# A layer of state space and experts: edge decays in four matmuls, routing and sends cut into pieces of the chunk steps, first expert weights asked two pieces sooner

## The chip, the core and the metric

The kernel runs on one core of a Trainium2 chip. Its engines are TensorE (PE, matmuls and transposes), VectorE (DVE), ScalarE (ACT), GpSimd (POOL) and SyncE (SP, which here only issues transfers). The metric is the device time of one execution in microseconds (us), smaller is better. A kernel's time is the median of its runs; the profile shows one further execution.

## The reference

Two layers over 8 sequences of 512 tokens of width 256, all in float32. Layer 0 normalizes `x`, then adds two things to it: a bidirectional state space block (projection, a convolution of 4 taps, a scan over chunks of 128 tokens with 8 heads and both directions, a gate, an output projection) and a mixture of 8 experts in which every token goes to its best one. Layer 1 normalizes again and adds latent attention of 16 heads and a second mixture with two experts per token. Of layer 0, cut to what the change touches:

```python
# state space: A = -exp(A_log), dt = softplus(proj + dt_bias); per chunk and direction
A_cs = cumsum(A * dt)                     # over the 128 tokens of the chunk
Y = C B^T * exp(segsum(A*dt)) (x*dt)  +  C state * exp(A_cs)    # inside the chunk, and from the state
# experts
probs = softmax(xn @ Wr + br); gate = max(probs); idx = argmax(probs)
y = gate * (relu(xn @ W1[idx] + b1[idx]) @ W2[idx] + b2[idx])
```

`exp(A_cs)` is what the kernel calls the edge decay (`ex`): with it the carried state enters every token of a chunk.

## The kernel before

**Opening.** `norm_and_project` goes over the 8 sequences, normalizes the tokens into `xn`, keeps the transposed ones in DRAM (`xtd`), and projects them onto `dt` and the router's logits (`proj`). `route` then computes `dt` and `da` (the product with A), and routes the tokens: softmax, first maximum, `ranks` (two matmuls and a sum over the 32 token tiles), the slot of every token (`slot0`) and the expert of every block of 128 slots (`w_idx`). It ends with 32 indirect transfers from GpSimd (L407), the "sends": each writes 128 rows of `xn` to their slots in the DRAM tensor `xd0`. Next come the first sequence's convolution parts, `decays` (L418 to L425), the first two chunks' preparation, and `edges` (L427 to L438): for each sequence and direction four matmuls into 8 rows, an exponential, and a write to the DRAM tensor `exd`, from which a chunk reads its edge decays (`ex`, L841). `edges` takes its rows `e8` from the rotating buffers `row` (8 of them), which also hold the rows of the convolution and the token rows `xt`.

The opening is put in order by a scheduler.

**Chunk steps.** Under `manual_schedule` every engine gets its instructions in the order in which the program states them. There are 64 steps n, 8 per sequence; j is n % 8. Each step does one chunk of one direction: `segments` and `prepare` for the next ones (`seg`, `au`), `inside` (`yd`), `before` (`yoff`, `ex`, added to `yT`), `pairs` (`cbm`, `xdd`), `behind` (the state `st`), `weigh` (`mt`). `others(n)` adds, in up to three turns, work of the neighbouring sequences: convolution parts of the next one (`pj`, `cv`, `th`; j = 1 to 6), gate, norm and output of the last one (j = 0 to 4), tokens (`xp`, `xt`, `xdt`, `bp`; j = 7 and 0).

Between these calls, `fill(1)` takes one piece of the experts: the generator `blocks` has 39 blocks of 128 slots, and a block is five pieces: transposes of its rows (L474, copy L476), first product in two halves (`h_ps`, L486, evicted by ScalarE at L493 and by VectorE at L495), second product in two halves (`y_ps`, L499), the last with the bias and the write to `yd0`. `fetch(j)` reads a block's rows from `xd0` through SP (L457) and its weights `w1`, `w2` and biases `b12` by indirect transfers from GpSimd (L461); it is called for block j + 1 in the first piece of block j. There are four calls of `fill` in a step, from step 2 on. When the blocks are done, `fill` takes pieces of `late`, the opening of layer 1: weights, then per finished sequence four gathers (`yg`), and seven pieces which add the experts' result, normalize again (`xn`, L567), transpose (`tp`, L575) and project. The last eight steps have two more calls.

```python
                if begun:
                    fill(1)          # begun = n >= 2; four times in a step
```

**Layer 1** interleaves attention steps with its own routing, sends, experts and gathers; the change doesn't touch it.

Of the kernel before, what the change touches and what calls it, by code (L numbers as in the profile page):

```python
# [8 lines left out]
FP = mybir.dt.float32  # L9
I32 = mybir.dt.int32  # L10
AF = mybir.ActivationFunctionType
ALU = mybir.AluOpType
# [37 lines left out]
def bc(ap, axis, shape):  # L50

    return ap.unsqueeze(axis).to_broadcast(shape)
# [3 lines left out]
def tile_kernel(ctx: ExitStack, tc: tile.TileContext, t, out: bass.AP):  # L56
# [48 lines left out]
    xtd = dram.tile([B, P, KC, S], FP, name="xtd", tag="xtd")  # L105
    exd = dram.tile([B, 2, NH, S], FP, name="exd", tag="exd")
    fdd = dram.tile([B, NH, S], FP, name="fdd", tag="fdd")
# [202 lines left out]
    dt = l0c.tile(D3, FP, name="dt", tag="dt")  # L310
    da = l0c.tile(D3, FP, name="da", tag="da")
    gate = ctile("gate", [P, NTILE])
# [3 lines left out]
    dec_tok = l0c.tile([P, 2, NTILE, NH], FP, name="dec_tok", tag="dec_tok")  # L316
    dec_all = l0c.tile(D3, FP, name="dec_all", tag="dec_all")

# [5 lines left out]

    def route():
        pool, big = r0p, r0b
        proj = big.tile([P, NTILE, 2 * NH + NE], FP, name="proj0", tag="proj0")
        xTs = {}
# [65 lines left out]
        V.tensor_copy(slot0, slots_of(big, oh, rank, "a"))  # L394


        B3 = [P, NBLK, NE - 1]
# [4 lines left out]
        V.tensor_scalar(be, be, float(P), pidx, ALU.mult, ALU.add)  # L402
        V.tensor_copy(w_idx, be)

        sent = []
        for i in range(NTILE):
            one = G.indirect_dma_start(  # L407
                out=xd0, out_offset=bass.IndirectOffsetOnAxis(ap=slot0[:, i : i + 1], axis=0),
                in_=xn[:, i, :], in_offset=None, bounds_check=NBLK * P - 1, oob_is_err=False,
            )  # L410
            for other in sent:
                tc.declare_no_dep(one.ins, other.ins, reason="rows go to slots of their own")
            sent.append(one)

    def decays():
        dp = bank("dp", [P, 2, NTILE * NH], 0)
        for d in range(2):
            T.matmul(  # L418
                dp[:, d, :].rearrange("p (t h) -> p t h", h=NH), LOW[d], da[:, :, d * NH : (d + 1) * NH],
                start=True, stop=True,  # L420
            )
        A.activation(dec_tok.rearrange("p d t h -> p d (t h)"), dp, AF.Exp)
        ta = bank("ta", [P, NTILE * 2 * NH], 0)
        T.matmul(ta, ones, da.rearrange(f2), start=True, stop=True)
        A.activation(dec_all.rearrange(f2), ta, AF.Exp)  # L425

    def edges():  # L427
        for b in range(B):
            for d in range(2):
                ct = bank("ct", [NH, S], 0)  # L430
                for c in range(TPB):
                    T.matmul(
                        ct[:, c * P : (c + 1) * P], da[:, b * TPB + c, d * NH : (d + 1) * NH], MSK[d],
                        start=True, stop=True,
                    )
                e8 = row("e8")
                A.activation(e8[:NH, :], ct, AF.Exp)
                Y.dma_start(out=exd[b, d], in_=e8[:NH, :])  # L438

    route()  # L440
    l1c = tl = w_r = rb = w_q = w_o = w_uk = w_uv = w_kv = band = slot1 = wsel = proj1 = vt0 = qk0 = r1b = noop = None
# [4 lines left out]
    with ExitStack() as es:  # L446
# [7 lines left out]

        def fetch(j):
            xd = e2.tile([P, DM], FP, name="xd", tag="xd", bufs=3)
            Y.dma_start(out=xd, in_=xd0[j * P : (j + 1) * P, :])  # L457
            got = [xd]
            for name, n, bufs in (("w1", KC * FF, 2), ("w2", FC * DM, 2), ("b12", FC + DM, 2)):
                w = e2.tile([P, n], FP, name=name, tag=name, bufs=bufs)  # L460
                G.indirect_dma_start(  # L461
                    out=w, out_offset=None, in_=t[name], bounds_check=NE * P - 1, oob_is_err=False,
                    in_offset=bass.IndirectOffsetOnAxis(ap=w_idx[:, j : j + 1], axis=0),
                )
                got.append(w)
            return got

        def blocks():
            got = fetch(0)
            for j in range(NBLK):  # L470
                xd, w1, w2, b12 = got
                tp = bank("xdT_ps", [P, DM], "e")
# [3 lines left out]
                A.copy(xdT, tp)  # L476
                if j + 1 < NBLK:
                    got = fetch(j + 1)
                yield
# [342 lines left out]
        class Chunk:  # L822
# [9 lines left out]
            def prepare(self):  # L832
                d = self.d
                self.au = p1.tile(H3, FP, name="au", tag="au")
                G.tensor_tensor(  # L835
                    self.au, bc(da[:, self.i, d * NH : (d + 1) * NH], 2, H3), bc(MSK[d], 1, H3), ALU.mult
                )
                if not self.first:
                    self.ex = p2.tile([P, HC, P], FP, name="ex", tag="ex", bufs=3)
                    for i in range(2):  # L840
                        Y.dma_start(  # L841
                            out=self.ex[HD * i : HD * (i + 1), :, :],
                            in_=bc(exd[self.b, d, i::2, self.cols], 0, [HD, HC, P]),
                        )
# [55 lines left out]
            def behind(self):  # L900
                if self.last:
                    return
                sp = bank("sp", [P, DI], "s")
                T.matmul(sp, self.bt.b_tok[self.c][:, self.d, :], self.xdd, start=True, stop=True)
                st = state[self.d]
                if self.first:
                    A.copy(st, sp)
                else:
                    d = self.d
                    G.tensor_tensor(  # L910
                        heads(st), heads(st), bc(dec_all[:, self.i, d * NH : (d + 1) * NH], 2, HP), ALU.mult
                    )
                    V.tensor_tensor(st, st, sp, ALU.add)
# [37 lines left out]
        batch[1].load()  # L951
        r0.close()
        xs.close()
        e2 = es.enter_context(tc.tile_pool(name="e2", bufs=2, side="right"))

        with tc.manual_schedule(engines=ENGINES):
# [31 lines left out]

            rows, rest = blocks(), late()

# [5 lines left out]
            for n in range(N):  # L996
# [6 lines left out]
                ahead = chunk[n + 1] if n + 1 < N else None  # L1003
                begun = n >= 2

# [14 lines left out]
                if begun:  # L1020
                    fill(1)
                now.before()
                if ahead:
                    ahead.pairs(batch[ahead.b])
                if begun:
                    fill(1)
# [4 lines left out]
                if begun:  # L1031
                    fill(1)
                while work:
                    turn()
                if n >= N - 8:
                    fill(2)
# [512 lines left out]
```

## Time and profile before

| | |
|---|---|
| median of 3 runs | 2250.88 us (2246.86 to 2252.46) |
| the profiled execution | 2233.12 us, span 2231.4 us, mean granted TensorE clock 0.922 |
| TensorE busy | 1935.2 us, 87% of the span |
| VectorE, ScalarE, GpSimd busy | 1499.0, 1070.2 and 689.8 us |
| 56 to 112 us | TensorE 33.2 of 56 us busy, clock 0.82; VectorE 44.6; GpSimd 5.7 |
| 112 to 168 us | TensorE 30.3 of 56 us busy, clock 0.73; VectorE 20.5; GpSimd 39.2 |
| 168 to 224 us | TensorE 51.9 of 56 us busy, clock 0.97 |
| 235 to 937 us | TensorE 668.6 of 702 us busy, clock 0.99 |
| 937 to 1175 us | TensorE 182.4 of 238 us busy, clock 0.84 |

The span runs from the first to the last instruction of one execution. The first chunk step begins at 169.8 us (its `yd`), block 0's first product at 191.4, the last block ends in step 50 near 944, the last step's `yd` is at 1147, and layer 1's first scores are at 1174.7. In a timeline line the columns are start, duration, engine, line, operation, out<-in, shape and count, and in brackets how long the engine was idle before it and what ended that. A matmul's end is modelled, so start-to-start distances are the better measure of what it costs TensorE. In a line of waits the numbers are the total in us, how often, and the longest.

### The profile page before, as it was taken

What the parts mean: (1) busy time and instruction counts of PE and PEld (TensorE: products, weight loads), DVE (VectorE), ACT (ScalarE), POOL (GpSimd) and SP (SyncE); (2) the same over time, 40 slices, a digit from 0 to 9 for tenths busy, and PEclk for the clock granted to TensorE, in tenths of its full rate; (3) what the DMA queues carried; (4) which work ended last, traced back from release to release, by engine and by line L of the source; (5) the groups of instructions that cost most, each with busy time, mean ns of one, the idle gap of its engine ahead of it and who ended that gap; (6) DMA issues with size and microseconds to landing.
All of it is one profiled execution on the core that took longest, in us unless ns stands there. A gap on an engine that the chain in (4) does not pass through costs nothing. (4 is left out here: it accounts for less than half of the span.)

```text
span 2231.4 us, 32949 instructions
## 1 busy us (share of the span) xinstructions
PE 1935.2 (87%) x11772; PEld 1281.0 (57%) x11772; DVE 1499.0 (67%) x3323; ACT 1070.2 (48%) x1978; POOL 689.8 (31%) x588
## 2 busy tenths in 40 slices
PE   6559999999998999987867768899999999999885
PEld 5325666667766676644544334565656656565543
DVE  4835766657585665678646679565666767676895
ACT  2223332323233242333324546676667777777764
POOL 0075554546364463655420035200000000000452
PEclk9879999999999999997885878799999999999978
DMA  7134544545454464343432161312213222222255
GB/s 263 38 103 160 174 157 162 193 141 203 139 172 150 132 212 143 128 128 114 157 100 67 37 212 61 96 53 84 71 46 101 82 67 78 58 86 58 90 110 97
DMA packets 156357, 263.61 MB, mean 118 GB/s; under 512 B 25146, under 2 KB 112622, under 8 KB 144290
## 3 DMA queue, kind: packets, MB, share of 16 engines
q1 hardware_dynamic: 124544, 144.65, 20.9%
q0 software_dynamic: 22320, 107.55, 14.9%
q10 hardware_dynamic: 9330, 9.31, 1.2%
q8 instruction: 93, 1.52, 0.3%
q14 instruction: 70, 0.57, 0.1%
HBM read 193.39 MB, written 72.75 MB: 119 GB/s over the span
## 5 line engine op out<-in xcount | busy, mean ns | idle before, releaser
L1289 DVE TENSOR_SCALAR s<-s_ps 128x512 f32<-128x512 f32 x512 | 317.4, 681 | 255.9 <-PE s_ps L1284 209.0
L1299 ACT ACTIVATE s<-s,ng 128x512 f32<-128x512 f32 x512 | 355.3, 727 | 51.7 <-DVE ng L1295 50.1
L1306 PE MATMUL p_ps<-ident,s 128*128 128x128 f32 x2048 | 296.0, 289 | 60.5 <-ACT pT L1307 60.5
L1306 PEld LDWEIGHTS p_ps<-ident,s 128*128 128x128 f32 x2048 | 244.7, 147 | 143.7 <-ACT pT L1307 94.3
L1291 DVE CUSTOM_DVE_ANT_0 s<-s,band 128x512 f32<-128x512 f32 x512 | 322.3, 683 | 0.0
L1307 ACT COPY pT<-p_ps 128x512 f32<-128x512 f32 x512 | 277.8, 591 | 56.3 <-PE p_ps L1306 52.1
L1249 POOL DMA_INDIRECT yg<-yd,at x64 | 67.6, 1056 | 700.6 <-PE s_ps L1284 654.3
L667 PE MATMUL pj<-xT,w_in 128*128 128x512 f32 x384 | 194.6, 632 | 19.4 <-DVE cv L680 18.3
L1284 PE MATMUL s_ps<-kT,qT 16*128 16x512 f32 x1024 | 181.5, 706 | 22.6 <-DVE s L1289 16.5
L486 PEld LDWEIGHTS h_ps<-xdT,w 128*128 128x128 f32 x1248 | 151.6, 195 | 32.6 <-issue 18.0
L486 PE MATMUL h_ps<-xdT,w 128*128 128x128 f32 x1248 | 156.7, 280 | 9.4 <-ACT xdT L476 8.3
L499 PE MATMUL y_ps<-w,hT 128*128 128x256 f32 x624 | 149.3, 382 | 0.7 <-DVE hT L495 0.7
L680 DVE SCALAR_TENSOR_TENSOR cv<-pj,w_conv_w,cv 128x511 f32<-128x511 f32 (+2 forms) x192 | 143.1, 745 | 7.4 <-ACT cv L676 3.4
L1315 PE MATMUL o_ps<-pT,vt 128*32 128x256 f32 x2048 | 143.2, 424 | 0.0
L898 POOL TENSOR_TENSOR yT<-yT,ex 128x512 f32<-128x512 f32 (+1 forms) x48 | 59.4, 1237 | 254.1 <-DVE ex L897 191.6
L499 PEld LDWEIGHTS y_ps<-w,hT 128*128 128x128 f32 x624 | 116.9, 192 | 35.7 <-issue 20.3
L887 DVE TENSOR_TENSOR yT<-yT,yd 128x512 f32<-128x512 f32 (+1 forms) x64 | 43.7, 682 | 122.6 <-PE yd L878 122.5
L667 PEld LDWEIGHTS pj<-xT,w_in 128*128 128x128 f32 x384 | 71.6, 200 | 92.1 <-issue 81.9
L1151 PE MATMUL e_hp<-e_xdT,e_w 128*128 128x256 f32 x448 | 122.4, 396 | 2.3 <-ACT e_xdT L1145 1.9
L835 POOL TENSOR_TENSOR au<-da,row_le 128x1024 f32<-128x1024 f32 x32 | 62.5, 1954 | 195.0 <-DVE end L387 94.1
L1164 PE MATMUL e_yp<-e_w,e_hT 128*128 128x256 f32 x448 | 120.0, 390 | 0.2
L855 ACT ACTIVATE mt<-seg 128x1024 f32<-128x1024 f32 x64 | 65.6, 1024 | 106.7 <-PE seg L850 106.6
(261 smaller groups left out, 3219.0 us busy)
## 6 DMA issues: line engine op xcount, KB each, us to landing
ex<-exd SPq DMA_DIRECT2D x96, 128.0 KB
u<-in_u_dram SPq DMA_DIRECT2D x16, 512.0 KB
xtd<-xT SPq DMA_DIRECT2D x16, 512.0 KB
fr<-fdd SPq DMA_DIRECT2D x64, 128.0 KB
od<-os SPq DMA_DIRECT2D x32, 256.0 KB
xT<-xtd SPq DMA_DIRECT2D x15, 512.0 KB
e_w<-in_ei_dram SPq DMA_DIRECT2D x7, 1024.0 KB
e_w<-in_eo_dram SPq DMA_DIRECT2D x7, 1024.0 KB
```

The costliest lines, as they stand in the source:

```text
L486: T.matmul(hp[:, i, :], w1[:, k * FF + f * P : k * FF + (f + 1) * P], xdT[:, k * P : (k + 1) * P], start=(k == 0), stop=(k == KC - 1),)
L499: T.matmul(yp, hT[f // 4][:, f % 4, :], w2[:, f * DM : (f + 1) * DM], start=(f == 0), stop=(f == FC - 1))
L667: T.matmul(pj, w_in[:, k, o * P : (o + 1) * P], self.xT[:, k, :], start=(k == 0), stop=(k == KC - 1))
L680: V.scalar_tensor_tensor(cv[:, s:], pj[:, : S - s], conv_w[:, q, 3 - s : 4 - s], cv[:, s:], ALU.mult, ALU.add)
L1151: T.matmul(hp, w1[:, k, f * P : (f + 1) * P], xdT[:, k, :], start=(k == 0), stop=(k == KC - 1))
L1284: T.matmul(sp[i], self.q[r, cols], self.k[r, :], start=True, stop=True)
L1289: V.tensor_scalar(self.p[i], sp[i], -CLAMP, CLAMP, ALU.max, ALU.min)
L1291: V.tensor_tensor_reduce(out=self.p[i], in0=self.p[i], in1=band[:, at : at + S], scale=1.0, scalar=-3.0e38, op0=ALU.mult, op1=ALU.max, acc ...
L1299: A.activation(self.p[i], self.p[i], AF.Exp, bias=self.ng[:, i : i + 1])
L1306: T.transpose(pp[:, k, :], self.p[i][:, k * P : (k + 1) * P], ident)
L1307: A.copy(pT[i][:, :, cc * P : (cc + 1) * P], pp)
L1315: T.matmul(op[32 * i : 32 * i + 32, half * 2 * P : (half + 1) * 2 * P], self.v[:, k, h * (AD + 1) : h * (AD + 1) + 32], pT[i][:, k, :], st ...
```

## The change

1. `da` and `dec_all` change their layout from token tile by direction and head to direction by token tile by head. One multiplication becomes two.
2. `edges` makes, for each direction and half of the token tiles, one matmul with 128 columns (16 tiles by 8 heads) into one bank; one exponential and one write follow. `exd` has the new layout, and L841 reads it there.
3. `route` is split: `steps` keeps the projection, `dt` and `da`; `route0` is a generator with the routing in six pieces and the sends in 16 pieces of two. The two matmuls of `ranks` use a bank of the experts' kind.
4. `fill` takes `route0`'s pieces first, then those of `blocks`. It is called in every step from 0 on, and a fifth time, at the end, in the first three steps of each sequence (j < 3). The pools of the opening are closed and the experts' pool opened inside `blocks`.
5. `fetch` asks by name. Block j + 1's `b12` and `w2` are asked for in the first piece of block j, as before; the rows and `w1` of block j + 2 in the fourth piece of block j, which is two pieces sooner than before.

```diff
+    exd = dram.tile([4, P, P], FP, name="exd", tag="exd")
+    EDGE = P // NH
...
-    da = l0c.tile(D3, FP, name="da", tag="da")
+    da = l0c.tile([P, 2, NTILE, NH], FP, name="da", tag="da")
...
-        V.tensor_tensor(da, dt, bc(ea, 1, D3), ALU.mult)
+        for d in range(2):
+            of = slice(d * NH, (d + 1) * NH)
+            V.tensor_tensor(da[:, d], dt[:, :, of], bc(ea[:, of], 1, [P, NTILE, NH]), ALU.mult)
+
+    def route0():
+        big = r0b
         pr = softmax_experts(big, proj[:, :, 2 * NH :], br)
+        yield
         m, oh = first_max(big, pr, "a")
         V.tensor_copy(gate, m)
-        rank, n = ranks(big, bank, oh)
+        yield
+        rank, n = ranks(big, lambda name, shape, tag: bank(name, shape, "e"), oh)
+        yield
...
         for i in range(NTILE):
...
+            if i % 2:
+                yield
...
     def edges():
-        for b in range(B):
-            for d in range(2):
-                ct = bank("ct", [NH, S], 0)
-                for c in range(TPB):
-                    T.matmul(
-                        ct[:, c * P : (c + 1) * P], da[:, b * TPB + c, d * NH : (d + 1) * NH], MSK[d],
-                        start=True, stop=True,
-                    )
-                e8 = row("e8")
-                A.activation(e8[:NH, :], ct, AF.Exp)
-                Y.dma_start(out=exd[b, d], in_=e8[:NH, :])
+        ct = bank("ct", [P, 4, P], 0)
+        for d in range(2):
+            for g in range(2):
+                T.matmul(
+                    ct[:, 2 * d + g, :], da[:, d, EDGE * g : EDGE * (g + 1), :].rearrange("p t e -> p (t e)"), MSK[d],
+                    start=True, stop=True,
+                )
+        e8 = row("e8").rearrange("p (g l) -> p g l", l=P)
+        A.activation(e8, ct, AF.Exp)
+        Y.dma_start(out=exd.rearrange("g p l -> p g l"), in_=e8)
...
         def blocks():
-            got = fetch(0)
+            nonlocal e2
+            r0.close()
+            xs.close()
+            e2 = es.enter_context(tc.tile_pool(name="e2", bufs=2, side="right"))
+            fetch(0, "xd", "w1", "b12", "w2")
+            fetch(1, "xd", "w1")
+            yield
             for j in range(NBLK):
...
-                if j + 1 < NBLK:
-                    got = fetch(j + 1)
+                fetch(j + 1, "b12", "w2")
                 yield
...
                     if f == 3:
+                        fetch(j + 2, "xd", "w1")
                         yield
...
-            rows, rest = blocks(), late()
+            rows, rest = itertools.chain(route0(), blocks()), late()
...
-                begun = n >= 2
...
-                if begun:
-                    fill(1)
+                fill(1)
...
                 while work:
                     turn()
+                if n % 8 < 3:
+                    fill(1)
```

More of the change, by code (lines that the diff above doesn't have):

```diff
@@ L1 @@
+import itertools
 from contextlib import ExitStack
@@ L105, in tile_kernel @@
     xtd = dram.tile([B, P, KC, S], FP, name="xtd", tag="xtd")
-    exd = dram.tile([B, 2, NH, S], FP, name="exd", tag="exd")
+    exd = dram.tile([4, P, P], FP, name="exd", tag="exd")
+    EDGE = P // NH
     fdd = dram.tile([B, NH, S], FP, name="fdd", tag="fdd")
@@ L316, in tile_kernel @@
     dec_tok = l0c.tile([P, 2, NTILE, NH], FP, name="dec_tok", tag="dec_tok")
-    dec_all = l0c.tile(D3, FP, name="dec_all", tag="dec_all")
+    dec_all = l0c.tile([P, 2, NTILE, NH], FP, name="dec_all", tag="dec_all")
     def bank(name, shape, tag="gen"):
@@ L323, in row, with steps @@
         return m2.tile([P, S], FP, name=name, tag="row", bufs=8)
-    def route():
+    proj = r0b.tile([P, NTILE, 2 * NH + NE], FP, name="proj0", tag="proj0")
+    def steps():
         pool, big = r0p, r0b
-        proj = big.tile([P, NTILE, 2 * NH + NE], FP, name="proj0", tag="proj0")
         xTs = {}
@@ L403, in route @@
         V.tensor_copy(w_idx, be)
+        yield
         sent = []
@@ L413, in route @@
             sent.append(one)
+            if i % 2:
+                yield
     def decays():
@@ L418, in decays @@
             T.matmul(
-                dp[:, d, :].rearrange("p (t h) -> p t h", h=NH), LOW[d], da[:, :, d * NH : (d + 1) * NH],
+                dp[:, d, :].rearrange("p (t h) -> p t h", h=NH), LOW[d], da[:, d],
                 start=True, stop=True,
@@ L423, in decays @@
         ta = bank("ta", [P, NTILE * 2 * NH], 0)
-        T.matmul(ta, ones, da.rearrange(f2), start=True, stop=True)
-        A.activation(dec_all.rearrange(f2), ta, AF.Exp)
+        T.matmul(ta, ones, da.rearrange("p d t e -> p (d t e)"), start=True, stop=True)
+        A.activation(dec_all.rearrange("p d t e -> p (d t e)"), ta, AF.Exp)
     def edges():
-        for b in range(B):
-            for d in range(2):
-                ct = bank("ct", [NH, S], 0)
-                for c in range(TPB):
-                    T.matmul(
-                        ct[:, c * P : (c + 1) * P], da[:, b * TPB + c, d * NH : (d + 1) * NH], MSK[d],
-                        start=True, stop=True,
-                    )
-                e8 = row("e8")
-                A.activation(e8[:NH, :], ct, AF.Exp)
-                Y.dma_start(out=exd[b, d], in_=e8[:NH, :])
-    route()
+        ct = bank("ct", [P, 4, P], 0)
[8 more added lines that the diff above has]
+        Y.dma_start(out=exd.rearrange("g p l -> p g l"), in_=e8)
+    steps()
     l1c = tl = w_r = rb = w_q = w_o = w_uk = w_uv = w_kv = band = slot1 = wsel = proj1 = vt0 = qk0 = r1b = noop = None
@@ L452, in heads, with fetch @@
             return ap.rearrange("p (h e) -> p h e", e=HD)
[L455 to L466, printed above, removed]
-        def blocks():
-            got = fetch(0)
+        def fetch(j, *names):
+            if j < NBLK:
+                for name in names:
+                    n, bufs = {"xd": (DM, 3), "w1": (KC * FF, 2), "w2": (FC * DM, 2), "b12": (FC + DM, 2)}[name]
+                    w = held[name, j] = e2.tile([P, n], FP, name=name, tag=name, bufs=bufs)
+                    if name == "xd":
+                        Y.dma_start(out=w, in_=xd0[j * P : (j + 1) * P, :])
+                    else:
+                        G.indirect_dma_start(
+                            out=w, out_offset=None, in_=t[name], bounds_check=NE * P - 1, oob_is_err=False,
+                            in_offset=bass.IndirectOffsetOnAxis(ap=w_idx[:, j : j + 1], axis=0),
+                        )
+        held = {}
+        def blocks():
+            nonlocal e2
[4 more added lines that the diff above has]
+            fetch(1, "xd", "w1")
+            yield
             for j in range(NBLK):
-                xd, w1, w2, b12 = got
+                xd, w1, w2, b12 = (held.pop((name, j)) for name in ("xd", "w1", "w2", "b12"))
                 tp = bank("xdT_ps", [P, DM], "e")
@@ L835, in prepare @@
                 G.tensor_tensor(
-                    self.au, bc(da[:, self.i, d * NH : (d + 1) * NH], 2, H3), bc(MSK[d], 1, H3), ALU.mult
+                    self.au, bc(da[:, d, self.i, :], 2, H3), bc(MSK[d], 1, H3), ALU.mult
                 )
@@ L839, in prepare @@
                     self.ex = p2.tile([P, HC, P], FP, name="ex", tag="ex", bufs=3)
+                    at = self.i % EDGE * NH
                     for i in range(2):
@@ L842, in prepare @@
                             out=self.ex[HD * i : HD * (i + 1), :, :],
-                            in_=bc(exd[self.b, d, i::2, self.cols], 0, [HD, HC, P]),
+                            in_=bc(exd[2 * d + self.i // EDGE, at + i : at + NH : 2, :], 0, [HD, HC, P]),
                         )
@@ L910, in behind @@
                     G.tensor_tensor(
-                        heads(st), heads(st), bc(dec_all[:, self.i, d * NH : (d + 1) * NH], 2, HP), ALU.mult
+                        heads(st), heads(st), bc(dec_all[:, d, self.i, :], 2, HP), ALU.mult
                     )
@@ L951, in tile_kernel @@
         batch[1].load()
-        r0.close()
-        xs.close()
-        e2 = es.enter_context(tc.tile_pool(name="e2", bufs=2, side="right"))
+        e2 = None
         with tc.manual_schedule(engines=ENGINES):
@@ L1015, in tile_kernel @@
                     pending.append(beginning)
-                if begun:
-                    fill(1)
+                fill(1)
                 now.inside()
                 turn()
-                if begun:
-                    fill(1)
+                fill(1)
                 now.before()
@@ L1024, in tile_kernel @@
                     ahead.pairs(batch[ahead.b])
-                if begun:
-                    fill(1)
+                fill(1)
                 turn()
@@ L1030, in tile_kernel @@
                     ahead.weigh()
-                if begun:
-                    fill(1)
+                fill(1)
                 while work:
                     turn()
+                if n % 8 < 3:
+                    fill(1)
                 if n >= N - 8:
```

## The prediction

> **What bounds the kernel now.** I read the page's slices first, then the timeline of each engine from 70 to 250 us (where the moved work lies), then TensorE's waits over the chunk steps, then one chunk step in detail. In the 40 slices (55.8 us each) TensorE is nearly full from slice 4 to 16; the holes are slices 1 and 2 and the stretch after slice 16.
>
> ```profile
> PE   6559999999998999987867768899999999999885
> POOL 0075554546364463655420035200000000000452
> PEclk9879999999999999997885878799999999999978
> ```
>
> TensorE's timeline shows what fills slice 2, and where the steps begin:
>
> ```profile
> 141.17 1.04 PE L432 MATMUL ct<-row_ge,da 128*8 128x128 f32 x8
> 158.05 1.88 PE L432 MATMUL ct<-row_le,da 128*8 128x128 f32 x8 [15.84 <-ACT e L437]
> ...
> 169.76 1.10 PE L878 MATMUL yd<-mt,xdt 128*64 128x128 f32 x16
> ...
> 191.36 2.02 PE L486 MATMUL h_ps<-xdT,w 128*128 128x128 f32 x16 [0.90 <-ACT cv L676]
> ...
> 200.43 1.88 PE L850 MATMUL seg<-au,row_gt 128*128 128x512 f32 x4
> ```
>
> GpSimd's timeline gives the cause: 32 sends in one row, and the token products queued behind them.
>
> ```profile
> 110.15 1.20 POOL L407 DMA_INDIRECT xd<-xn,slot  x1 [2.43 <-DVE slot L394]
> ...
> 152.49 0.97 POOL L407 DMA_INDIRECT xd<-xn,slot  x1 [0.30 <-issue]
> 153.48 1.92 POOL L835 TENSOR_TENSOR au<-da,row_le 128x1024 f32<-128x1024 f32 x1
> 155.33 2.05 POOL L745 TENSOR_TENSOR xdt<-xt,dt 128x512 f32<-128x512 f32 x2
> ```
>
> The edge rows (`e8`) take the same rotating row buffers as the token rows that L745 has still to read, so ScalarE, TensorE and the first chunk step (169.76) stand still. After that the steps follow TensorE: from 235 to 937 us it is busy 668.6 of 702, and its waits for other engines sum to 32.9 us, the largest being these:
>
> ```profile
> PE bp L751 <- DVE z L764: 8.7, 4, 2.9
> PE h_ps L486 <- ACT xdT L476: 8.3, 6, 2.2
> PE yd L878 <- DVE mt L872: 6.4, 5, 1.8
> PE pj L667 <- DVE cv L680: 5.4, 4, 2.7
> ```
>
> There is no wait for a weight transfer among them. So a stall put into these steps adds to the end almost in full.
>
> **What the Trainium skill says.** "PSUM — Partial Sum Buffer", *Engine vs sequencer instructions*: the queues of ScalarE, VectorE and GpSimd are strictly first in, first out, and matmuls start in program order. The trace agrees: 16 us of ScalarE and TensorE behind one GpSimd row. "ScalarE: Activation LUTs", *What ACT_TABLE_LOAD costs*: 1283 ns a load, plus a drain; the trace has 1283 ns, and no drain beside it. "TensorE: Matmul & The Clock Gate", *What's actually happening*: an idle TensorE falls to half clock; here `pj` takes 3.48 us at 186.98, after a wait of 2.96, against 1.88.
>
> **The change part by part.** 64 `ct` matmuls of 8 columns become 4 of 128, and 16 exponentials (587 ns) and 16 writes become one each. With the sends gone from ahead of L745 this wait ends. The first step then hangs on VectorE: from 71.8 us it has left softplus (about 15 us as listed there), 8 convolution parts (three taps at 0.66 and a product at 0.60: 20.6), the start of the first batch (four at 0.60, eight at 0.66: 7.7) and mask and weighting (1.4): 44.7, with some 5 us of waits for convolution evictions and the 1.4 for the exponential: 122 us. The routing's 15 us or so, interleaved there before, are gone from it. **Step 0 starts at 122 instead of 170.**
>
> The routing is not gone but now stands between steps 0 and 1: softmax 1.1, first maximum 2.2, two matmuls about 2, ranks 3.1, one weighting 1.2, then slots 3.7, with the adds between: slots at about 137 (before: 109.8). From there GpSimd paces the steps. Until block 0's first weights it issues 32 sends at 1.28 (41.0), four `au` (1.9), three `yT` (1.1), four `xdd` and three `st` (1.04): 59, so it asks for them at about 195. Nothing takes them off its queue: L461 and the xd load on SP both stand behind the last send. Before, the first `h_ps` came 6.5 us after the ask at 184.8; now **about 202 instead of 191.4**. But it now stands in step 5 and not in step 2. Three steps lie between `seg` at 200.43 and `seg` at 244.81, 44.4 us, which hold 12 block pieces still to be done: two blocks and two pieces. By start-to-start times (`h_ps` 1.79 twice, `y_ps` 1.73 twice, transposes 0.22) a block is 7.26, so 16.5. Gain: 44.4 - 16.5 - 10.6 = 17.3, less about 1 for cold-clock matmuls in steps 1 to 4: **-16 us**.
>
> The 12 pieces are made up by a fifth call of `fill` in the first three steps of each batch, 35 pieces a batch, exactly seven blocks; 218 pieces end in step 49 where 195 ended in step 50. The block order is therefore the same in every batch: in its first three steps (j = 0, 1, 2; steps 8, 9, 10, then 16, 17, 18, and so on) the fourth call is the transposes `xdT_ps` and the fifth the first `h_ps`, and the built instruction order has nothing between them on TensorE. That is 16 places (six j = 0, five each of j = 1 and 2). `h_ps` waits for ScalarE's copy L476, and everything on TensorE waits behind it. Step 10 of the kernel before has this very order of ScalarE:
>
> ```profile
> 317.62 0.78 ACT L676 ACTIVATE cv<-pj,w_conv_b,w_conv_w 128x512 f32<-128x512 f32 x1 [5.57 <-PE pj L667]
> 318.42 1.28 ACT L159 ACT_TABLE_LOAD   x1
> 319.71 0.20 ACT L159 ACTIVATE rq_s<-ms 128x4 f32<-128x4 f32 x1
> 319.94 1.28 ACT L684 ACT_TABLE_LOAD   x1
> 321.23 0.63 ACT L684 ACTIVATE th<-cv 128x512 f32<-128x512 f32 x1
> 321.77 0.35 ACT L476 COPY xdT<-xdT_ps 128x256 f32<-128x256 f32 x1
> ```
>
> ```profile
> 318.22 0.38 PE L474 MATMUL xdT_ps<-ident,xd 128*128 128x128 f32 x2
> 318.44 1.88 PE L850 MATMUL seg<-au,row_gt 128*128 128x512 f32 x4
> ```
>
> There `seg` and `op` (3.4 us) covered the copy. Without them TensorE stands from 318.44 to 322.0: 3.5 us at j = 2. At j = 1 the copy stands behind `th` of the second convolution and the state copy: from the end of its `pj`, second `y_ps`, bias add, product, three taps, `th`, state, copy end 8.2 us later, while TensorE is ready at 5.6: 2.6. At j = 0 it stands behind `z`, `b_tok` and the state copy: 1.75. Together 6 x 1.75 + 5 x 2.6 + 5 x 3.5 = 41 us. Against it I set old waits that these take over: the 8.3 for the copy, the 5.4 for `cv` (it follows j = 2), a quarter of the mt row: 15. **+26 us**. Unseen in the trace is how far the other engines catch up meanwhile; the bare delay (matmul 0.38 + copy 0.37 - 0.22) is about 0.6, the highest seen in step 10's form 3.7, so the pairs cost 10 to 50 and I take 41.
>
> The weights asked for two pieces sooner: 0. No wait for them shows before; cover gone it would be the 6.5 us from ask to matmul, once, and that is counted above. The later ask also waits on `h_ps` two pieces back, which TensorE has passed; GpSimd's `au` has a step of slack behind it.
>
> The end of the layer: second-layer pieces start a step sooner, and steps 56 to 58 do seven each. That puts one normalization's four pieces into one step three times, the form which made TensorE wait 7.05 + 3.28 for `xn` at 1044; steps 60 and 63 are lighter for it. From 937 to 1175 TensorE waits 27.9 for `xn` as it is. I take 0, between -8 and +15. The second layer itself starts with the same work left.
>
> Sum: -16 + 26 + 0 = +10 us on the profiled execution (span 2231.4, its own time 2233.1, so 2243). The median of the runs, 2250.9, lies 17.8 above that execution; carried over, **2261**.
>
> **Rivals.** *The pairs are cheap* (faster, 0.22): ScalarE is early, each pair costs the bare 0.6, 10 in all, and the 15 still vanish: -16 + 10 - 15 = -21, so 2230. It decides wherever the pairs average under 1 us (16 x 1.0 = 16 breaks even without the credit). For it: of some ten places before where only `yoff` and `cb` lay between copy and use, most show no wait. Against it: the ScalarE order above. *Half of both* (0.18): 20 - 5 - 16 = 0, 2251. *The tail pays too* (0.20): the three packed normalizations cost 5 each beyond the mean case, +25, 2276. *It does not do what it says*: GpSimd's row would have to stay ahead of the first step; the built order excludes it.
>
> **How the numbers follow.** The likeliest case (0.40) gives 2261, its own range 2251 to 2271. With the rivals, 2232 to 2281 leaves about 0.1 on each side. A measurement here can tell about 0.3% (6.8 us) from no change: the cheap pairs give faster 0.20; half of both and the low end of the likeliest, same 0.25; the rest slower 0.55.
>
> **What would show it.** Right: first `yd` near 122 us; first `h_ps` near 202 in step 5; GpSimd solid from 137 to 195; TensorE's wait for L476's copy at some 35 to 45 us over 16 places, largest where the table loads are. Wrong: that wait under 16 us; the first `h_ps` after 212, or before 192; a new row of waits for `w`; the wait for `xn` far from 28.

## The result, and the profile after

The changed kernel takes 2316.1 us (median of 4 runs, 2306.8 to 2339.2); the kernel before took 2250.5 beside it (2246.9 to 2252.5). The ratio is 1.030, with a 95% interval of 1.025 to 1.035: 3.0% slower. The forecast had the sign, but 2316 lies far outside its range of 2232 to 2281. The profiled execution of the changed kernel has a span of 2305.1 us, 73.7 more than the 2231.4 of before, and a mean granted clock of 0.912 instead of 0.922.

The start times of `yd` cut the span into four stretches. In the first three, the amount of expert work done differs between the kernels, so it is priced with the start-to-start times of the prediction (a half of `h_ps` 1.79 us, of `y_ps` 1.73, transposes 0.22):

| stretch | before | after | difference | expert work that differs | net |
|---|---|---|---|---|---|
| start to `yd` of step 8 | 280.8 | 257.0 | -23.8 | after has done 4 halves of `h_ps`, 6 of `y_ps` and 2 pairs of transposes less: 18.0 | -6 |
| `yd` of step 8 to step 48 | 629.1 | 700.0 | +70.9 | after does 6 halves of each and 3 pairs of transposes more: 21.8 | +49 |
| `yd` of step 48 to step 63 | 237.3 | 256.4 | +19.1 | after has 2 halves of `h_ps` and a pair of transposes less to do: 3.8 | +23 |
| `yd` of step 63 to the end | 1084.2 | 1091.8 | +7.6 | none | +8 |

The prediction's sum had -16, +26 and 0 in the first three rows, +10 in all; they came to +66.

**The middle stretch.** TensorE's waits between `yd` of step 8 and `yd` of step 48:

```profile
PE h_ps L512 <- ACT xdT L503: 53.0, 20, 3.6
PE bp L778 <- DVE z L791: 4.6, 5, 0.9
```

Two rows, 57.6 us. Before, the same steps had eight rows which sum to 28.4, and this was the copy's (L476 there):

```profile
PE h_ps L486 <- ACT xdT L476: 6.6, 5, 2.2
```

In the changed kernel the row for `z` has shrunk from 8.7 to 4.6 and the others are gone: 23.8 us of the old waits have disappeared. Idle time still rose by 29.2. This is how an adjacent pair (transposes, and the first `h_ps` right behind them) looks at j = 2, TensorE's timeline and then ScalarE's:

```profile
444.27 1.02 PE L932 MATMUL sp<-xdd,b_tok 128*128 128x512 f32 x2
445.12 0.38 PE L501 MATMUL xdT_ps<-ident,xd 128*128 128x128 f32 x2
449.08 3.54 PE L512 MATMUL h_ps<-xdT,w 128*128 128x128 f32 x16 [3.57 <-ACT xdT L503]
```

```profile
444.53 0.78 ACT L703 ACTIVATE cv<-pj,w_conv_b,w_conv_w 128x512 f32<-128x512 f32 x1 [5.57 <-PE pj L694]
445.33 1.28 ACT L162 ACT_TABLE_LOAD   x1
446.62 0.20 ACT L162 ACTIVATE rq_s<-ms 128x4 f32<-128x4 f32 x1
446.84 1.28 ACT L711 ACT_TABLE_LOAD   x1
448.14 0.63 ACT L711 ACTIVATE th<-cv 128x512 f32<-128x512 f32 x1
448.67 0.35 ACT L503 COPY xdT<-xdT_ps 128x256 f32<-128x256 f32 x1
```

It is the order of ScalarE that the prediction quoted from step 10 of before: two table loads and `th` ahead of a copy of 0.35 us. The prediction gave this pair 3.5 us; it waits 3.57. What the prediction left out stands in the duration of the `h_ps` line: 3.54 us, where the second half of the block takes 1.95 (at 455.90). After the idle time TensorE runs on slowly: the trace's granted clock over these 3.5 us is 0.55. Of the 20 first halves of `h_ps` behind a wait in this stretch, 14 ran at a granted clock of 0.50 to 0.79 and took 2.50 to 3.78 us; the other 6 had 1.00 and took 2.05. The slow clock reaches the matmuls behind `h_ps` too:

```profile
L512 PE MATMUL h_ps<-xdT,w 128*128 128x128 f32 x1121 | 157.0, 299 | 53.0 <-ACT xdT L503 53.0
L878 PE MATMUL seg<-au,row_gt 128*128 128x512 f32 x80 | 43.7, 675 | 0.0
L878 PE MATMUL seg<-au,row_lt 128*128 128x512 f32 x80 | 39.6, 619 | 0.0
```

These are groups of the changed kernel in the same stretch (busy us, mean ns of one, idle before), and these the groups of the kernel before:

```profile
L486 PE MATMUL h_ps<-xdT,w 128*128 128x128 f32 x1024 | 129.0, 280 | 6.8 <-ACT xdT L476 6.6
L850 PE MATMUL seg<-au,row_gt 128*128 128x512 f32 x80 | 37.6, 593 | 0.0
L850 PE MATMUL seg<-au,row_lt 128*128 128x512 f32 x80 | 37.6, 592 | 0.0
```

Of the 49 us, 29 are more idle time, and the other 20, by subtraction, are matmuls that run slower.

**The start.** GpSimd's row of sends begins late, and its end sets the first weights (GpSimd's timeline):

```profile
144.92 1.20 POOL L423 DMA_INDIRECT xd<-xn,slot  x1 [6.58 <-DVE slot L408]
...
186.78 1.06 POOL L938 TENSOR_TENSOR st<-st,dec_all 128x512 f32<-128x512 f32 x1
...
204.79 1.55 POOL L482 DMA_INDIRECT w<-in_w_dram,w_idx  x1 [1.25 <-DMA xd<-xn,slot]
```

The prediction had 137 for the first and 195 for the last. The middle line is a thing that it counted as 1.04 us of GpSimd's time and followed no further: the decay of the carried state stands between sends, VectorE's sum `st` waits 7.23 us for it, the mask product `mt` stands behind that, and `yd` of step 4 waits 8.57 us:

```profile
187.87 0.69 DVE L941 TENSOR_TENSOR st<-st,sp 128x512 f32<-128x512 f32 x1 [7.23 <-POOL st L938]
188.47 1.22 DVE L900 TENSOR_TENSOR mt<-mt,cbm 128x1024 f32<-128x1024 f32 x1
189.75 1.55 PE L906 MATMUL yd<-mt,xdt 128*64 128x128 f32 x12 [8.57 <-DVE mt L900]
```

In steps 0 to 4 `yd` waits 26.4 us for `mt`, and steps 3 to 6 come 17 to 19 us after the step ahead of them.

**The end of layer 0.** From `yd` of step 48 to the end of the chunk steps, the largest wait of TensorE is this one:

```profile
PE tp L602 <- DVE xn L594: 41.5, 7, 10.0
```

In the kernel before it was this:

```profile
PE tp L575 <- DVE xn L567: 27.9, 7, 7.1
```

### The profile page after: what moved, and what is told of

It reads as the page before. It is cut to its first block, busy times and chain, and to the rows that moved or that the text cites. A ratio compares the mean times of both kernels' runs of the same rounds, so it can differ in the third digit from the quotient of the medians.

```text
span 2305.1 us, 32661 instructions
## 1 busy us (share of the span) xinstructions
PE 1944.9 (84%) x11652; PEld 1290.8 (56%) x11652; DVE 1468.9 (64%) x3324; ACT 1060.4 (46%) x1961; POOL 679.6 (29%) x588
## 3 DMA queue, kind: packets, MB, share of 16 engines
q0 software_dynamic: 22320, 107.55, 15.2%
## 5 line engine op out<-in xcount | busy, mean ns | idle before, releaser
L1329 PE MATMUL p_ps<-ident,s 128*128 128x128 f32 x2048 | 300.9, 291 | 80.2 <-ACT pT L1330 66.6
L512 PE MATMUL h_ps<-xdT,w 128*128 128x128 f32 x1248 | 173.1, 297 | 57.0 <-ACT xdT L503 56.7
L694 PE MATMUL pj<-xT,w_in 128*128 128x512 f32 x384 | 201.8, 652 | 12.9 <-DVE cv L707 12.8
L512 PEld LDWEIGHTS h_ps<-xdT,w 128*128 128x128 f32 x1248 | 164.0, 210 | 77.6 <-ACT xdT L503 61.6
L521 DVE TENSOR_SCALAR hT<-h_ps,b 128x128 f32<-128x128 f32 x156 | 43.9, 344 | 167.6 <-PE h_ps L512 167.6
L525 PEld LDWEIGHTS y_ps<-w,hT 128*128 128x128 f32 x624 | 115.4, 191 | 27.9 <-issue 15.8
L703 ACT ACTIVATE cv<-pj,w_conv_b,w_conv_w 128x512 f32<-128x512 f32 x64 | 49.7, 777 | 174.6 <-PE pj L694 174.6
L926 POOL TENSOR_TENSOR yT<-yT,ex 128x512 f32<-128x512 f32 (+1 forms) x48 | 56.4, 1175 | 223.7 <-DVE ex L925 121.7
```

The lines of the kernel that those rows point to most:

```text
L512: T.matmul(hp[:, i, :], w1[:, k * FF + f * P : k * FF + (f + 1) * P], xdT[:, k * P : (k + 1) * P], start=(k == 0), stop=(k == KC - 1),)
L525: T.matmul(yp, hT[f // 4][:, f % 4, :], w2[:, f * DM : (f + 1) * DM], start=(f == 0), stop=(f == FC - 1))
L694: T.matmul(pj, w_in[:, k, o * P : (o + 1) * P], self.xT[:, k, :], start=(k == 0), stop=(k == KC - 1))
L1329: T.transpose(pp[:, k, :], self.p[i][:, k * P : (k + 1) * P], ident)
```

## Experiments

They ran on four chips. The medians of the kernel before lay between 2229 and 2254 us there, so each kernel is told by its ratio to the kernel before on the same chip; the changed kernel itself has only its 1.030. One kernel (`merged`) had 0.990 on one chip and 0.997 on another, so ratios of different chips that lie less than about 0.7% apart are not told apart by themselves; there the traces have to speak. The theory was that the 22 places where a block's transposes are followed too closely by its first `h_ps` hold TensorE up, by the wait and by the slow matmuls after it. The main rival was that the later start of the blocks and the end of the layer carry the loss, and that the waits at the pairs only show slack which would otherwise show elsewhere.

**The same pieces, one call later.**

```diff
             if i % 2:
                 yield
+        yield
```

> One empty piece between the sends and the blocks: every block piece comes one call later, nothing else changes. In the built order no transposes then stand directly ahead of their first h_ps; at least 1.1 us of other matmuls lie between, mostly 2.5. Theory (the adjacent pairs hold TensorE up, by the wait and by the half-speed matmuls after it): the wait for the xdT copy falls from 56.7 us to under 15, h_ps and seg lose the 24 us by which they ran slower, some 10 us of old waits (z, cv, mt) come back: about 55 us less than the changed kernel's 2316, so 2262 (2250 to 2275). Rival (the pairs only show slack that other waits would show in their place; the later start and the tail of the layer carry the loss): at most 20 us less, 2296 or more.

Measured: ratio 0.996 (0.993 to 0.999), 2218.3 us beside 2230.0. One empty piece takes away 3.4%, more than the change had cost and more than the 55 us expected. TensorE's waits in steps 8 to 48:

```profile
PE bp L779 <- DVE z L792: 14.4, 5, 2.9
PE h_ps L513 <- ACT xdT L504: 3.8, 5, 0.8
PE y_ps L526 <- ACT hT L520: 2.7, 4, 0.7
```

The wait for the copy is gone, 10 us of old waits for `z` are back, and this stretch takes 639.7 us instead of 700.0. `h_ps` needs 138.1 us for the same 1121 matmuls instead of 157.0, and both `seg` are at 593 ns. The rest of the gain, 16 us in the profile, is at the end of the layer: TensorE waits 20.9 us for `xn` and not 41.5, and the stretch from step 48 to 63 takes 240.2. I had not foreseen that part. The rival falls: nothing was changed but the place of the pieces in a step (their requests and evictions move with them), and the blocks start no sooner (first `h_ps` at 215.8 instead of 211.6).

**TensorE kept busy through the waits.**

```diff
                     hp = bank("h_ps", [P, FC // 2, P], "e")
+                    if half == 0 and n >= 6 and n % 8 in (0, 1, 2, 6):
+                        for _ in range({0: 9, 1: 10, 2: 15, 6: 9}[n % 8]):
+                            T.matmul(hp[:, 0, :], w1[:, :P], ident, start=True, stop=True)
```

> The changed kernel with matmuls of no use put in front of the first h_ps of a block in steps with j = 0, 1, 2 and 6 (9, 10, 15 and 9 of 128x128, 2.0 to 3.4 us, just under the waits there, into a bank that the real ones start anew). TensorE has as much to wait for as before, but does not idle. Theory (of the pairs' cost some 24 us is clock: h_ps and seg at half speed after each wait): the wait for the xdT copy falls to some 10 us, h_ps and seg come back to the duration of the kernel before, and the time falls by 20 us, to 2296 (2288 to 2304). Rival (the slow matmuls are not due to the idle time, or what they lose is made up elsewhere): within 6 us of 2316.

Measured: 1.021 (1.017 to 1.024), where the changed kernel had 1.030 (1.025 to 1.035): 0.9%, or 21 us, as forecast, though across chips. The traces are firmer: the stretch from step 8 to 48 takes 673.8 us instead of 700.0. The added matmuls fill the time in which TensorE would stand, so no work is saved. The granted clock in this stretch is 1.00, where it was 0.96 in the changed kernel and 0.99 before. The durations follow:

```profile
L515 PE MATMUL h_ps<-xdT,w 128*128 128x128 f32 x1121 | 139.7, 278 | 5.0 <-ACT xdT L503 5.0
L511 PE MATMUL h_ps<-ident,w 128*128 128x128 f32 x430 | 51.3, 275 | 0.0
L881 PE MATMUL seg<-au,row_gt 128*128 128x512 f32 x80 | 37.6, 593 | 0.0
```

Useless matmuls, 51.3 us of them, make the kernel faster (the trace counts two passes for each, hence 430). So some 20 to 26 us of the pairs' cost (20 by the subtraction above, 26 by this stretch) is the clock after the wait and not the wait itself.

**No fifth call.**

```diff
-                if n % 8 < 3:
-                    fill(1)
```

> The changed kernel without the fifth call of fill in the first three steps of a batch: 32 pieces a batch, so the order of the blocks turns from batch to batch and no pair is adjacent, but blocks end some five steps later (step 54). Theory (pairs): 55 us less for the pairs, 5 to 15 more for block pieces that now stand in the last ten steps: 2271 (2258 to 2285), the wait for the xdT copy under 15. Rival (start and tail carry the loss): 2296 or more.

Measured: 0.997 (0.995 to 0.999). Again more than expected. The last step's `yd` comes at 1122 us, 25 before that of the kernel before, but more of the second layer's pieces are then still to do, and TensorE waits 57.0 us for `xn` in all. With `one_later` this says that the fifth call itself is harmless; which two pieces meet around it is what counts.

**The edges alone**, in the kernel before: the new `edges`, with the layouts of `da`, `dec_all` and `exd`, and `route` left where it was.

> The kernel before with the first part of the change alone: edge decays in four matmuls, one exponential, one write; routing and sends stay in the opening. Theory (in the kernel before, the 16 edge rows wait for row buffers that the token products hold, and those stand behind the 32 sends): the token products still start at about 155, but ScalarE and TensorE no longer stand, first yd at about 160 instead of 170; the first weights are asked for as before (GpSimd): 2242 (2232 to 2250). Rival (the first steps hang on the token products and on the weights alone): 2250 within 4. Stronger rival (the row wait is all of the opening's cost): first yd before 145, 2230 or less.

Measured: 1.000 (0.998 to 1.002). The first `yd` comes at 156.6 instead of 169.8, near the 160 expected, but steps 2 to 8 are only 5 us earlier than before and the last step 2. The 17.0 us in which TensorE stood before at `ct`, for the exponentials and their row buffers, has become this:

```profile
PE yd L882 <- POOL xdt L748: 21.5, 1, 21.5
```

A wait that was taken away uncovered the next one, for the token products behind the sends, and after it 9.4 us for `mt` in three places where there had been 5.0. My 2242 was too hopeful; the weaker rival was right.

**The fifth call in the first six batches only.**

```diff
-                if n % 8 < 3:
+                if n % 8 < 3 and n < 48:
```

> The changed kernel with the fifth call of fill in the first six batches only: the blocks keep their order up to step 47 and end a step later, but steps 48 to 58 make three to five fewer calls for the second layer's pieces. In the changed kernel the stretch from step 48 to the last yd costs 19 us more than before, with the wait for xn at 41.5 us instead of 28. Theory (steps of seven calls put a whole normalization into one step, and that is what the 13 us are): the wait for xn falls below 32, and the ratio to the kernel before falls from 1.030 by 0.5 to 0.8 of a per cent, to 1.023 (1.019 to 1.027). Rival (it is only where the pieces stand against the step, not how many there are): ratio 1.030 within 0.003, wait for xn 36 or more.

Measured: 1.029 (1.022 to 1.035), and TensorE waits 43.4 us for `xn`. The interval of the ratio still reaches the 1.023 of the theory, but the wait is far from its 32, so the theory falls: three steps of seven calls are not what costs at the end of the layer.

**Only the second layer's pieces one call later.**

```diff
+            yield
             yield from second_weights()
```

> The changed kernel with one empty piece between the last block and the first piece of the second layer: the blocks and their pairs stand as they are, only the second layer's pieces come one call later. Theory (the 19 us that the last 15 steps cost more than before come from where these pieces stand in the step: a piece that normalizes and the piece that transposes its result meet in two calls with nothing between; the kernel one_later, which has the same shift, waits 21 us for xn there and loses 3): the wait for xn falls from 41.5 to about 21, the blocks' waits stay at 53 to 57, ratio 1.024 (1.019 to 1.027). Rival (the tail is late because it starts late, and the waits are filled by other ones): 1.030 within 0.003.

Measured: 1.024 (1.021 to 1.027), as the theory had it. The same row of the same stretch:

```profile
PE tp L603 <- DVE xn L595: 19.5, 5, 6.1
```

The pairs are untouched (53.0 us in steps 8 to 48), and the stretch from step 48 to 63 takes 235.6 us instead of 256.4. With the 3.8 us of expert work that differ, all but 2 us of the +23 are gone, so it came from where the second layer's pieces stand in the step. It looks like the same matter as the pairs: at the longest wait of the changed kernel (9.96 us, up to 1119.43) VectorE goes through a whole normalization from 1108.23 on, while TensorE has nothing but `seg` to do ahead of the transposes that need the result. That it is this and nothing else about the place was not tested.

**The weights asked sooner, alone**, in the kernel before (`fetch` as in the change, nothing else).

> The kernel before with the last part of the change alone: xd and first weights of a block asked for two pieces sooner. Theory (no wait for weights stands in the steps, so nothing can be gained, and the issue on GpSimd costs the same): ratio 1.000 within 0.002. Rival (the first weights of block 1 now stand on GpSimd ahead of other work in steps 2 and 3, or the transfers collide): 1.003 or more.

Measured: 0.993 (0.990 to 0.996), so 0.7% faster, where I had said no change and the rival had said slower. The kernel before shows a place where it comes from, at its step 35. GpSimd, then VectorE:

```profile
694.25 1.04 POOL L461 DMA_INDIRECT w<-in_w_dram,w_idx  x1 [1.04 <-issue]
695.60 0.99 POOL L461 DMA_INDIRECT w<-in_w_dram,w_idx  x1 [0.30 <-issue]
696.89 1.01 POOL L461 DMA_INDIRECT b<-in_b_dram,w_idx  x1 [0.30 <-DMA ex<-exd]
697.93 1.05 POOL L910 TENSOR_TENSOR st<-st,dec_all 128x512 f32<-128x512 f32 x1
```

```profile
699.01 0.69 DVE L913 TENSOR_TENSOR st<-st,sp 128x512 f32<-128x512 f32 x1 [5.73 <-POOL st L910]
699.62 2.30 DVE L872 TENSOR_TENSOR mt<-mt,cbm 128x1024 f32<-128x1024 f32 x1
```

Three requests of 1.3 us each stand ahead of the state decay; VectorE waits for that, and `yd` at 701.97 waits 1.80 us for `mt`. With the requests split, this place has two of them:

```profile
686.79 1.05 POOL L464 DMA_INDIRECT b<-in_b_dram,w_idx  x1 [0.15 <-ACT cv L680]
688.15 0.99 POOL L464 DMA_INDIRECT w<-in_w_dram,w_idx  x1 [0.30 <-issue]
689.17 1.05 POOL L914 TENSOR_TENSOR st<-st,dec_all 128x512 f32<-128x512 f32 x1
```

and `yd` follows without a wait at 693.51. In steps 8 to 48 the four waits of `yd` for `mt`, 4.9 us in the kernel before, are gone altogether, and the stretch takes 618.6 us instead of 629.1.

**The requests split, but none sooner**, in the kernel before: `xd` and `w1` where they stood, `w2` and `b12` after the first half of `h_ps`.

```diff
-                if j + 1 < NBLK:
-                    got = fetch(j + 1)
+                fetch(j + 1, "xd", "w1")
                 yield
...
+                    if half == 0:
+                        fetch(j + 1, "w2", "b12")
                     yield
```

> The kernel before with the three weight requests of a block split, but none sooner: xd and w1 where they stood, w2 and b12 one piece later. In the kernel before GpSimd issues three requests in a row (3.8 us) 14 times ahead of an au and 5 times ahead of a state decay; with split_only (0.993) such rows are of one or two. Theory (that gain is GpSimd's row ahead of au and of the state decay, behind which VectorE's state sum, mask product and TensorE's yd wait; when the weights land counts for nothing): most of the gain again, 0.995 (0.992 to 0.998), and no wait of yd for mt in steps 8 to 48. Rival (asked sooner is what gains): 1.000 within 0.002.

Measured: 0.996 (0.994 to 0.998). Two of the three requests now come later than before, none sooner, and 0.4 of the 0.7% are still there; `yd` waits for `mt` once, 1.3 us. So a gain comes from GpSimd's row alone, without any sooner landing of weights. The two intervals overlap and the chips differ, so whether the other 0.3% is due to asking sooner stays open.

**The routing computed in the opening, the sends in the steps** (on top of two empty pieces, which give the blocks the order of `one_later`).

```diff
     steps()
+    routing = route0()
+    for _ in range(6):
+        next(routing)
...
-            rows, rest = itertools.chain(route0(), blocks()), late()
+            rows, rest = itertools.chain(routing, blocks()), late()
```

> As one_later (no adjacent pairs, 0.996 of the kernel before), but the routing is computed in the opening again (slots ready at about 110 us), and only the 32 sends are pieces, from step 0 on; the blocks keep one_later's order and start five calls sooner. Theory (the first weights are asked for when GpSimd is through its row, and that row starts when the slots are ready: 144.9 to 204.8 in the changed kernel): first yd at about 142 instead of 127, GpSimd's row ends at about 187, first h_ps at about 196 instead of 215.8, steps 1 to 4 closer together; ratio 0.991 (0.986 to 0.995). Rival (the 15 us of the later first step are lost in full, as TensorE is what bounds): ratio 0.998 or more.

Measured: 1.002 (0.999 to 1.005). This didn't test what it was meant to. The sends begin only 3 us sooner, because on GpSimd they stand behind token products which wait for ScalarE:

```profile
131.95 2.95 POOL L777 TENSOR_TENSOR xdt<-xt,dt 128x512 f32<-128x512 f32 x2 [14.37 <-ACT xt L774]
134.86 1.49 POOL L900 TENSOR_TENSOR xdd<-xdt,dec_tok 128x512 f32<-128x512 f32 x1
136.31 5.47 POOL L777 TENSOR_TENSOR xdt<-xt,dt 128x512 f32<-128x512 f32 x4
141.96 1.20 POOL L423 DMA_INDIRECT xd<-xn,slot  x1 [0.18 <-DVE yT L920]
```

141.96 instead of 144.92, and the first `h_ps` is at 208.4, not at 196.

**A block in four pieces**: no fifth call, and the transposes of the next block issued at the head of a block's last piece, so that the second half of `y_ps` and then `seg` cover every copy (`turned` makes the transposes and the copy; the rest of the edit is left out here).

```diff
                     if f == 3:
                         fetch(j + 2, "xd", "w1")
                         yield
+                        if j + 1 < NBLK:
+                            xdT = turned(j + 1)
...
-                if n % 8 < 3:
-                    fill(1)
```

> The changed kernel without the fifth call, and with a block's transposes issued in the last piece of the block before it (ahead of its second y_ps), so that a block is four pieces, one block a step, and between transposes and first h_ps lie the second y_ps, seg and more (3.4 to 5.2 us of matmuls) in every step; blocks end in step 44. Theory (pairs and cold clock are the loss, and the blocks' place is free): waits for the xdT copy zero, h_ps 155 us busy or less; as no_fifth at the start, and the tail has more steps for the second layer's pieces: ratio 0.990 (0.984 to 0.996). Rival (VectorE and ScalarE then hold up the fuller steps: new waits for z, mt and cv of 30 us and more): 1.000 or more.

Measured: 0.990 (0.984 to 0.996). No wait for the copy is left.

**The same with the routing in the opening, side by side with it.**

```diff
     steps()
+    for _ in route0():
+        pass
...
-            rows, rest = itertools.chain(route0(), blocks()), late()
+            rows, rest = blocks(), late()
```

The calls of `fill` begin at n = 2 again, and two empty pieces keep the blocks' place in a step.

> As merged (a block in four pieces, one block a step), but with the routing and its 32 sends in the opening, ahead of the first step, as in the kernel before; the blocks stand at the same places of a step and start three steps sooner. Theory (the start's gain of 16 us is not there: what the earlier first step wins, GpSimd's row of sends in the steps takes back): the same as merged within 0.4 of a per cent, 0.990. Rival (the start is worth the 16 us forecast): 0.007 slower than merged, 0.997 or more.

> The kernel merged beside merged_opening on one chip: 0.990 (0.985 to 0.995).

Measured on one chip: 0.992 (0.989 to 0.994) with the routing in the opening, 0.997 (0.996 to 0.998) with it in the steps. The second is worse than the 0.990 of the run before, and outside what I expected; both of them are faster than the kernel before. At `yd` of step 7 the kernel with the routing in the steps is 21.5 us ahead (235.20 against 256.65), and has done 6 halves of `h_ps`, 6 of `y_ps` and three pairs of transposes less, which is 21.8 us. So moving the routing and its sends into the steps wins nothing at the start. The 0.5% arises later, and is explained only in part. Of the 15.2 us between the two profiles, 4.7 are there at the last `yd` of layer 0: the blocks that started sooner end sooner, and in the last 15 steps TensorE waits 6.7 us for `xn` instead of 18.7. Another 11.0 lie between the first scores of layer 1 and the end (1051.0 us against 1062.0), where both kernels have the same program; no run here says why. The kernel with four pieces to a block and the routing in the opening is the faster one of the two on this chip, some 0.8% faster than the kernel before.

## Why the prediction failed

**The pairs: the mechanism right, the term too small.** The prediction set 41 us for 16 places at j = 0, 1 and 2, and a credit of 15. Those places have 12.7 + 12.7 + 17.9 = 43.3 us of waits in the trace; per place it had 1.75, 2.6 and 3.5 and the trace has 2.24 (1.5 in step 48), 2.54 and 3.57. Three things were off. First, j = 6: there the transposes stand in the second call and `h_ps` in the third with only `yoff` and `cb` between, which the prediction took for cover since most such places before showed no wait. Six more places, 13.4 us. Second, the matmuls after a wait: 20 to 26 us (`keep_warm`). The prediction charged "about 1 for cold-clock matmuls" to the first steps and nothing to the pairs, though it had quoted 3.48 instead of 1.88 us for `pj` after a wait of 2.96. That line of the trace was what to work the pairs out with. The Trainium skill's page "TensorE: Matmul & The Clock Gate", *What's actually happening*, on which the prediction drew, sets the half clock after an idle window of about 3.4 us; by that figure alone only the pairs at j = 2 would have been in question, while in these traces waits of 2.2 us were enough. Third, against these two, the credit was 23.8 us rather than 15; a part of it isn't the pairs' doing, since the waits for `mt` also vanish with the split requests alone. Together +49 instead of +26.

**The start: -6 instead of -16.** The steps of the working are in the trace, each somewhat late: first `yd` 127.2 (122), slots at 144.4 (137), first weights at 204.8 (195), first `h_ps` in step 5 at 211.6 (202). These 9.6 us are about what is missing of the 16. VectorE needed 17.5 us for the routing between other work, beginning 5 us later. About 5 of the 6 us that are won come from the new edges (`edges_only` is 5 us ahead of before at steps 2 to 8), and the moved routing nets nothing (`merged_opening` against `merged_5`). GpSimd was indeed solid until the last send, but of what stood in its queue behind the sends only the weights were followed, and not the state decay, on which VectorE's `mt` and so `yd` hang.

**The end of the layer: +23 instead of 0.** "From 937 to 1175 TensorE waits 27.9 for `xn` as it is. I take 0" was the step that failed. The rival *the tail pays too* had named the place and the sign, with the packing of three normalizations as its cause; `fifth_48` shows that the packing isn't it, and `late_shift` that the place in the step is. The prediction followed every call of a step for the pieces of the blocks; for the second layer's pieces, which go through the same calls, it counted only how many fall into a step.

**The weights sooner: -0.7% in the kernel before instead of 0.** The reason given, that no wait for weights shows, was true and beside the point: a request costs GpSimd 1.3 us whoever waits for its data, and three in a row delay what stands behind them. "GpSimd's `au` has a step of slack behind it" looked at the wrong neighbour: in the lines at 694 to 698 it is the state decay that comes late, and `yd` with it. `split_only`, the last part of the change alone, has 0.993, and the whole change with its pieces moved (`one_later`, 0.996) or without the fifth call (`no_fifth`, 0.997) is no faster. As far as ratios of different chips can tell, nothing is left for the edges and the moved routing.

**Not settled.** The second layer took 7.6 us more in the changed kernel's profile. `keep_warm` and `late_shift`, whose second layer is the same, took 1080.7 and 1081.0 us there, against 1084.2 of before, so it is probably not of the change; on other chips, this is no proof. How far this stretch moves by itself shows in `split_only`, whose second layer is that of the kernel before: 1120.3 us, at a granted clock of 0.87 from the first scores on, against 0.91 before.

The range failed because each rival varied one term with the others at their likeliest. The two that lost, the pairs and the end of the layer, are both set by the phase between a period of five calls and a step of four or five, and so they could move together.

## What to carry to other kernels

Where pieces are dealt out in fixed places of a loop, list for every residue which producer and consumer become neighbours on the bounding engine, of every kind of piece that goes through these places, before pricing anything else: here one empty piece was worth 3.4%. Price a stall of the matmul engine with the slow matmuls after it, as well as with the wait. An asynchronous request is paid where it is issued: look at what stands behind it in that queue, not only at who waits for its data.

## What the runs showed of the hardware

- After idle times of 2.2 to 3.6 us the next 16 `h_ps` matmuls took anything from 2.05 to 3.78 us. A wait of 2.54 us was followed by 3.62 us at 284.76 and by 2.05 at 850.04, and one of 3.57 us by 3.78 at 306.72 and by 2.05 at 870.36. The granted clock goes with it: 0.53 and 1.00 over the first two of these, 0.50 and 1.00 over the other two. The Trainium skill's page "TensorE: Matmul & The Clock Gate", *What's actually happening*, says that an idle window of about 3.4 us, which runs freely, brings the half clock. Such variation fits a window that runs freely, but here 2.2 us of standing were enough in some places: at 232.44 and 796.04, after 2.19 us, the 16 matmuls took 2.59 and 2.96 us.
- An issue of an indirect transfer kept GpSimd busy for about 1.0 us (694.25 to 697.90 above: 1.04, 0.99, 1.01), and the next one began 1.3 us after its start.
- A mask product `mt` on VectorE takes 1.22 us (188.47 in the changed kernel), but 2.30 in the lines above at 699.62; GpSimd's `au` ran at the same time there (698.93 to 700.83).
